# A matmul-bound expert layer on one core: SyncE's transfers are ordered behind the product that precedes them in the source

## The chip, the core and the metric

The kernel runs on one core of one Trainium2 chip. The core has a matmul engine (TensorE, PE in the profile; its weight loads are listed apart as PEld), three engines for elementwise work (VectorE or DVE, ScalarE or ACT, GpSimd or POOL) and SyncE (SP), which here only issues DMA transfers. Each engine takes its instructions in one fixed order. Where an instruction needs another engine's result it waits on a semaphore, and everything behind it on that engine waits too. The metric is the device time of one execution in microseconds (us).

## The reference

The input x has 8 rows of 512 positions with 256 features. There are eight experts and one shared expert, each a gated MLP of width 1024. All in float32, cut to what is computed:

```
for e in 0..7 and the shared one:
    H_e   = silu(x @ Wg[e]) * (x @ Wu[e])        # 8 x 512 x 1024
    out_e = H_e @ Wd[e]                          # 8 x 512 x 256
mixed = sum over e < 8 of gates[b, e] * out_e
out   = x + (1 - s[b]) * mixed + s[b] * out_shared
```

`gates` and `s` hold one number per row b (and expert); they sit in the tile `coef`.

## The kernel before

**Units.** The eight rows are taken in two halves of four (`h`), the nine experts in turn (`e`), and the 1024 hidden features in two halves (`g`). That gives 2 x 9 x 2 = 36 *units*. A unit holds four rows and four blocks of 128 hidden features, so for the gate (m = 0) and the up matrix (m = 1) it has 4 x 4 results of 128 x 512, each over 256 features, two products of depth 128. The kernel spares some of these: for each of the six pairs (i, j) in `PAIRS` it gets the two results (i, j) and (j, i) from three products instead of four. It uses differences and sums of the operands for that. The forms of x (`v`, a difference, and `b`, two sums) come from scratch tensors in DRAM in nearly all units; the forms of the weights (`u`, `wb`, `at`) are made by GpSimd in each unit. The down projection is treated in the same way (`ud`, `wd`, `ad`; `rows` and `cols` are sums of hidden tiles that GpSimd adds up, line 579).

**The order on the matmul engine** is written out by hand as a string for each unit:

```
HUB = "GGD" * 8
BLOCK = "GGDGGDGGD"
ORDER = HUB + BLOCK * 6
```

G is one gate or up product of this unit (`gate_up`, lines 831 to 916), D one down product (`down`, lines 608 to 731). The D's of the *hub* and the first D's after it still belong to the unit before. The hub does the four "diagonal" results (`P_step`, `Q_step`). Block p (p = 0 to 5) then does pair p: for m = 0 and m = 1 it has `R1_step` of pair p + 1 (line 542, uses `v` and `u`) and two `R_step`s of pair p (line 552, use `b` and `wb`). A unit has 26 D's; I number them D1 to D26. D8 ends the hub and D11, D14, D17, D20, D23 and D26 end blocks 0 to 5.

**Where the transfers stand in the source.** All of them after the start are issued on SyncE:

- `x_difference(u, p + 3)`, line 298: `v` of pair p + 3, at the start of block p. Three buffers.
- `x_sums(u, p + 2)`, line 315: `b` of pair p + 2, right after the last `R_step` of block p. Two buffers, so it waits for that product.
- `load_w(nxt, p - 2)`, line 362: for p = 2 to 5, at the start of block p, the next unit's gate and up weights of feature block p - 2, as two transfers (gate first, then up). Five buffers of a tile `w`, four of which a unit holds.
- `make_at(nxt, p - 2)`, lines 369 to 385, directly behind it in the source for p = 3 and 4: GpSimd makes `at` from the weights just asked for.
- `load_d(nxt)`, line 409, at the start of block 5. The first transfers of a unit (`v` of pairs 0 to 2, `b` of pairs 0 and 1) stand at the start of its hub.

**Side jobs.** Two generators run along with the units; each `next` moves one a step. `prepare(1)` (lines 234 to 282) builds the forms of the second half's x in units 2 to 16. A step is taken after D8, D11, D14, D17 and D20 (`AHEAD_AT`); each of the four rows takes six steps (the first issues eight strided loads, line 173) and each of the six pairs eight steps (the first issues two loads of 512 KB, line 265, the eighth three stores of 256 KB, line 280). `close_rows(0)` (lines 754 to 797) finishes the first half's output from unit 20 on, a step after D5, D8, ..., D23 (`CLOSE_AT`): loads of kept sums (lines 762, 769, 771), VectorE operations on them (lines 775 to 792), four strided loads of x (line 738) and four stores (line 796) per row. Both use tiles of a pool of two buffers, `iopool`.

**Who sets the order.** TensorE's and GpSimd's instructions keep the source's order (`HAND`, line 942); ScalarE's do so in unit 0. Everything else is put in order by a planner that plays the program through with its own durations: each time an engine is free in that plan, it takes the first instruction in source order that is ready and whose buffer is free. So a SyncE transfer takes its place in SyncE's queue as soon as the plan has a buffer for it, however far ahead of its place in the source. The order is then fixed, and semaphores are put in where data or buffers need them.

Of the kernel before, what the change touches and what calls it, by code (L numbers as in the profile page):

```python
# [16 lines left out]
def kernel(  # L17
# [37 lines left out]
    nc = tc.nc  # L55
    B, S, D = x.shape
# [4 lines left out]
    NI = 4  # L61
# [35 lines left out]
    gp = nc.gpsimd  # L97
    ve = nc.vector

    def weights(e):  # L100
        return (Wg[e], Wu[e], Wd[e]) if e < E else (Sg, Su, Sd)

# [20 lines left out]
    scratch = {}  # L123
# [23 lines left out]
    def load_rows(pool, tag, b):  # L147
        rows = []
        for c in range(2):
            if pool is not iopool:  # L150
                t = pool.tile([P, 2, D], F32, tag=tag, name=f"xin{b}_{c}")
            elif c == 0:
                both = pool.tile([P, NT, D], F32, tag=tag, name=f"xin{b}")
            if pool is iopool:
                t = both[:, 2 * c : 2 * c + 2]
            nc.sync.dma_start(
                t, x[b].rearrange("(p t) d -> p t d", t=NT)[:, 2 * c : 2 * c + 2, :]
            )
            rows.append(t)
        return rows  # L160
# [6 lines left out]
    def load_turned(to, b):  # L167


        at = x[b].rearrange("(c r t) d -> r t c d", r=32, t=NT)  # L170
        for k in (1, 0):
            for q in range(4):
                nc.sync.dma_start(
                    to[k][ts(q, 32)].rearrange("r (t c d) -> r t c d", t=NT, d=32),
                    at[:, :, :, ts(4 * k + q, 32)],
                )
# [57 lines left out]
    def prepare(h):  # L234

        def tile_of(name):
            return iopool.tile([P, 2, S], F32, tag="io", name=f"{name}{h}")

        for i in range(NI):
            to = xdram[h, i] = dram.tile([P, 2, S], F32, tag=f"xd{h}_{i}", name=f"xd{h}_{i}")  # L240
            rows = [
                zpool.tile([P, S], F32, tag="z", name=f"xin{i}_{k}_{h}") for k in range(2)
            ]
            load_turned(rows, NI * h + i)
            yield
            yield
            both = tile_of(f"xt{i}_")
            for k in (1, 0):
                ve.transpose(both[:, k], rows[k])
                if k == 0 and CI[i] != 0.0:  # L250
                    ve.scalar_tensor_tensor(
                        both[:, 0], both[:, 1], -CI[i], both[:, 0], ALU.mult, ALU.add
                    )
                yield
            yield
            for k in (1, 0):
                nc.sync.dma_start(to[:, k], both[:, k])
            yield
        for p, (i, j) in enumerate(PAIRS):
            d = CI[i] - CI[j]  # L260
            to = dram.tile([P, 3, S], F32, tag=f"xs{h}_{p}", name=f"xs{h}_{p}")
            at = {}
            for n in (i, j):
                at[n] = tile_of(f"f{p}_{n}_")
                nc.sync.dma_start(at[n], xdram[h, n])
            yield
            yield
            v, B_i, B_j = at[i][:, 0], at[i][:, 1], at[j][:, 1]
            gp.tensor_tensor(v, v, at[j][:, 0], ALU.subtract)
            if d != 1.0:  # L270
                gp.tensor_scalar(v, v, 1.0 / d, 0.0, ALU.mult, ALU.add)
            yield
            gp.tensor_tensor(B_j, v, B_j, ALU.add)
            yield
            gp.tensor_tensor(B_i, v, B_i, ALU.add)
            yield
            yield
            yield
            for k, made in enumerate((v, B_j, B_i)):
                nc.sync.dma_start(to[:, k], made)  # L280
            scratch[h, p] = to
            yield

    def load_x(h, i):
        xhub[h, i] = xpool.tile([P, 2, S], F32, tag="x", name=f"x{h}_{i}")
        nc.sync.dma_start(xhub[h, i], xdram[h, i])

    def x_difference(u, p):

        i, j = PAIRS[p]  # L290
        v = vpool.tile([P, S], F32, tag="v", name=f"v{u.name}_{p}")
        if (u.h, p) not in scratch:
            d = CI[i] - CI[j]
            ve.tensor_sub(v, xhub[u.h, i][:, 0], xhub[u.h, j][:, 0])
            if d != 1.0:
                nc.scalar.mul(v, v, 1.0 / d)
        else:
            nc.sync.dma_start(v, scratch[u.h, p][:, 0])
        u.V[p] = v

    def x_sums(u, p):


        i, j = PAIRS[p]
        v = u.V[p]
        b = bpool.tile([P, 2, S], F32, tag="b", name=f"b{u.name}_{p}")
        if (u.h, p) not in scratch:
            ve.tensor_add(b[:, 0], v, xhub[u.h, j][:, 1])
            gp.tensor_tensor(b[:, 1], v, xhub[u.h, i][:, 1], ALU.add)
            scratch[u.h, p] = dram.tile(  # L310
                [P, 3, S], F32, tag=f"xs{u.h}_{p}", name=f"xs{u.h}_{p}"
            )
            u.store.append((scratch[u.h, p], v, b))
        else:
            nc.sync.dma_start(b, scratch[u.h, p][:, 1:3])
        u.VB[p] = b

    def store_forms(u):
        for to, v, b in u.store:
            nc.sync.dma_start(to[:, 0], v)  # L320
            nc.sync.dma_start(to[:, 1:3], b)
        u.store = []

    def touch_banks():
# [29 lines left out]
                u.ad, u.Ud, u.Wd = {}, {}, {}  # L354
                units.append(u)

    def load_w(u, i, queue=nc.sync):
        if i not in u.raw:
            u.raw[i] = wpool.tile([P, 2, 2, P], F32, tag="w", name=f"w{u.name}_{i}")
        t = u.raw[i]  # L360
        for m in range(2):
            queue.dma_start(
                t[:, m],
                weights(u.e)[m][:, ts(NI * u.g + i, P)].rearrange(
                    "(k p) f -> p k f", p=P
                ),
            )
# [38 lines left out]
    def load_d(u):  # L406
        t = dpool.tile([P, NI, D], F32, tag="wd", name=f"wd{u.name}")
        r0 = NI * u.g * P
        nc.sync.dma_start(
            t, weights(u.e)[2][r0 : r0 + NI * P].rearrange("(c p) d -> p c d", p=P)  # L410
        )
        u.raw_d = t
# [186 lines left out]
    def keep(u, acc, *keys):  # L599

        for key in keys:
            if key in acc:
                kept[key] = dram.tile(
                    [P, S], F32, tag=f"kept{key[0]}{key[1]}", name=f"kept{key[0]}{key[1]}"
                )
                nc.sync.dma_start(kept[key], acc[key])

    def down(u, acc):

# [123 lines left out]
    def load_back(h, i):  # L733

        if (h, i) not in back:
            xr = iopool.tile([P, S // 32, 2, 32], F32, tag="io", name=f"xr{h}_{i}")
            for q in range(4):
                nc.sync.dma_start(xr[ts(q, 32)], squares(x, NI * h + i, q))
            back[h, i] = xr
        return back[h, i]  # L740

# [12 lines left out]
    def close_rows(h):  # L754
# [4 lines left out]
        for i in range(NI):  # L759
            y = pair_of(f"y{i}")  # L760
            for r in range(2):
                nc.sync.dma_start(y[:, r], kept["bB"[r], i])
            yield
            for p, (k, j) in enumerate(PAIRS):
                if i not in (k, j):
                    continue
                s = (1.0 if i == k else -1.0) / (CI[k] - CI[j])
                vs = pair_of(f"vs{i}_{p}")
                nc.sync.dma_start(vs[:, 0], kept["V", p])
                if p in OWN:  # L770
                    nc.sync.dma_start(vs[:, 1], kept["S", p])
                yield
                yield
                if p in OWN:
                    ve.tensor_sub(vs[:, 0], vs[:, 0], vs[:, 1])
                    if i == k:
                        ve.tensor_sub(y[:, 1], y[:, 1], vs[:, 1])
                    yield
                ve.scalar_tensor_tensor(y[:, 0], vs[:, 0], s, y[:, 0], ALU.mult, ALU.add)
                yield  # L780
# [12 lines left out]
                )  # L793
                yield
            for q in range(4):
                nc.sync.dma_start(squares(out, NI * h + i, q), xr[ts(q, 32)])
            yield

    last_rows = {}
# [17 lines left out]
    def store_rows(j):  # L817
        b = NI * (NH - 1) + j
        for c, xr in enumerate(last_rows[j]):
            for t in (0, 1) if j == NI - 1 and c == 1 else (slice(0, 2),):  # L820
                if j in tails:
                    ve.tensor_add(xr[:, t], tails[j][c][:, t], xr[:, t])
                at = out[b].rearrange("(p c t) d -> p c t d", c=2, t=2)[:, c]
                nc.sync.dma_start(at[:, t], xr[:, t])

    HUB_STEPS = [
        (what[0], int(what[1]), int(what[2]))
# [116 lines left out]
    by_hand.enter_context(  # L944
        tc.manual_schedule(engines=HAND | {mybir.EngineType.Activation})
    )
    load_w(units[0], 0, nc.scalar)
    load_gates()
    touch_banks()
    loaded = []  # L950
# [13 lines left out]
    for u in units:  # L964
# [52 lines left out]
        if u.n + 2 == len(units):  # L1017
            for _ in closing:
                pass
        if u.n == 0:  # L1020
            by_hand.close()
            by_hand.enter_context(tc.manual_schedule(engines=HAND))
        for _ in turning:
# [38 lines left out]
```

## Time and profile before

| | |
|---|---|
| median of three runs | 2451.72 us (2451.71 to 2453.01) |
| the profiled execution's own time: its span, first to last instruction | 2451.5 us, 22846 instructions |
| PE (matmuls) busy | 2433.5 us, 99% |
| POOL busy | 2115.8 us, 86% |
| DVE busy | 1951.8 us, 80% |
| ACT busy | 1248.6 us, 51% |
| chain that ended last | PE 93%, DVE 3%, POOL 2%, DMA 1%, issue 1% |
| DMA | 267.10 MB, 109 GB/s; SyncE's queue 36.4% of 16 engines' span |
| granted TensorE clock | 1.000 |

Rows of the time line have the start, the duration (both in us), the engine, the source line, the operation with output and input tiles, and in brackets the idle time of that engine just before, with what ended it. SPq is SyncE issuing transfers. Rows of waits have the total, how often, and the longest. Rows of transfers have the count, the size and the median from issue to landing.

### The profile page before, as it was taken

Reading aid. Unit: us, or ns where it says so; the run is one execution under the profiler, and the core shown is the slowest. Engines: PE = TensorE matmul, PEld = TensorE weight load, DVE = VectorE, ACT = ScalarE, POOL = GpSimd, SP = SyncE. Lnnn points to the kernel's source line nnn. Section 1 sums busy time; section 2 is a strip of 40 time slices with the busy share of each in tenths; the row PEclk is TensorE's granted clock in tenths of the full one; section 3 lists DMA queues with packets and bytes.
Section 4 is the critical chain, followed back from the end, with each engine's and each line's share of the span. In section 5 each row is a group of like instructions: output and inputs, shape, how many; then the busy total and the mean of one; then the engine's idle time right before and its main releaser. Section 6 shows DMA issues by size and latency. Waiting matters only on the chain.

```text
span 2451.5 us, 22846 instructions
## 1 busy us (share of the span) xinstructions
PE 2433.5 (99%) x5726; PEld 1078.5 (44%) x5726; DVE 1951.8 (80%) x2881; ACT 1248.6 (51%) x2310; POOL 2115.8 (86%) x2339
## 2 busy tenths in 40 slices
PE   9999999999999999999999999999999999999999
PEld 4444444444444444444444444444444444444444
DVE  6777878777777877787787778888878787777787
ACT  4555555554555555555555555454554555555543
POOL 7988888898888989898888888898888888888885
PEclk9999999999999999999999999999999999999999
DMA  4333343343333333334553323434335343233332
GB/s 145 98 106 112 99 116 112 103 133 104 124 109 97 111 104 99 103 112 125 174 160 96 93 85 104 124 94 125 99 103 146 95 120 91 84 89 97 88 93 86
DMA packets 226129, 267.10 MB, mean 109 GB/s; under 512 B 64336, under 2 KB 156752, under 8 KB 226000
## 3 DMA queue, kind: packets, MB, share of 16 engines
q1 hardware_dynamic: 225168, 265.35, 36.4%
q8 instruction: 48, 0.79, 0.1%
q14 instruction: 81, 0.66, 0.1%
q10 hardware_dynamic: 832, 0.30, 0.0%
HBM read 245.14 MB, written 20.45 MB: 108 GB/s over the span
## 4 chain that ended last, share of the span: by engine, by line
PE 93%; DVE 3%; POOL 2%; DMA 1%; issue 1%; ACT 0%; ACTq 0%; SPq 0%; DVEq 0%; POOLq 0%
PE c L552 29%; PE c L542 15%; PE c L487 9%; PE c L464 9%; PE r L655 7%; PE r L693 7%; PE S L639 5%; PE b L639 5%; PE q L655 5%; PE s L655 2%; POOL cols L579 1%; POOL rows L579 1%; DVE h L455 0%; PE tail L812 0%; DVE P L480 0%
## 5 line engine op out<-in xcount | busy, mean ns | idle before, releaser
L552 PE MATMUL c<-b,wb 128*128 128x512 f32 x1720 | 843.7, 592 | 0.6 <-DMA b<-xs 0.6
L450 ACT ACTIVATE sg<-c 128x512 f32<-128x512 f32 x576 | 343.8, 597 | 585.8 <-DVE c L557 351.8
L455 DVE SCALAR_TENSOR_TENSOR h<-sg,coef,c 128x512 f32<-128x512 f32 x576 | 427.4, 742 | 240.5 <-PE c L552 132.7
L552 PEld LDWEIGHTS c<-b,wb 128*128 128x128 f32 x1720 | 326.4, 190 | 411.1 <-issue 389.1
L542 PE MATMUL c<-v,u 128*128 128x512 f32 x860 | 439.4, 592 | 2.0 <-POOL wb L403 1.5
L579 POOL TENSOR_TENSOR rows<-rows,h 128x512 f32<-128x512 f32 x282 | 372.7, 1322 | 0.0
L579 POOL TENSOR_TENSOR cols<-cols,h 128x512 f32<-128x512 f32 x282 | 363.6, 1289 | 0.0
L547 DVE TENSOR_TENSOR c<-D,c 128x512 f32<-128x512 f32 x430 | 297.5, 692 | 72.6 <-ACT sg L450 51.8
L557 DVE TENSOR_TENSOR c<-c,D 128x512 f32<-128x512 f32 x430 | 296.9, 690 | 17.5 <-PE c L552 17.2
L464 PE MATMUL c<-x,w 128*128 128x512 f32 x572 | 274.5, 592 | 0.0
L402 POOL TENSOR_TENSOR wb<-u,wb 128x256 f32<-128x256 f32 x108 | 79.3, 734 | 220.8 <-ACT wb L400 220.8
L542 PEld LDWEIGHTS c<-v,u 128*128 128x128 f32 x860 | 162.7, 190 | 209.1 <-issue 168.9
L568 DVE TENSOR_TENSOR X<-h,h 128x512 f32<-128x512 f32 x213 | 214.3, 1006 | 6.8
L655 PE MATMUL r<-h,wd 128*128 128x512 f32 x426 | 217.6, 592 | 1.3 <-DVE h L455 1.3
L693 PE MATMUL r<-X,ud 128*128 128x512 f32 x426 | 217.5, 592 | 0.0
L497 ACT COPY D<-c 128x512 f32<-128x512 f32 x284 | 166.0, 584 | 96.2 <-DVE h L455 96.2
L487 PE MATMUL c<-x,at 128*128 128x512 f32 x432 | 210.6, 595 | 3.4 <-DVE P L480 3.0
L579 POOL TENSOR_TENSOR rows<-h,h 128x512 f32<-128x512 f32 x144 | 200.0, 1389 | 0.0
L579 POOL TENSOR_TENSOR cols<-h,h 128x512 f32<-128x512 f32 x144 | 187.7, 1304 | 0.0
L470 ACT COPY P<-c 128x512 f32<-128x512 f32 x216 | 125.9, 587 | 109.2 <-PE c L464 104.9
L464 PEld LDWEIGHTS c<-x,w 128*128 128x128 f32 x572 | 108.4, 190 | 136.0 <-issue 111.9
L638 ACT COPY S<-accS 128x512 f32<-128x512 f32 x135 | 79.6, 590 | 147.9 <-DVE accV L626 146.9
(117 smaller groups left out, 3515.2 us busy)
## 6 DMA issues: line engine op xcount, KB each, us to landing
b<-xs SPq DMA_DIRECT2D x209, 512.0 KB, 3.6
v<-xs SPq DMA_DIRECT2D x209, 256.0 KB, 2.7
wd<-in_L_cond_Wd_dram SPq DMA_DIRECT2D x32, 512.0 KB, 5.0
w<-in_L_cond_Wg_dram SPq DMA_DIRECT2D x127, 128.0 KB, 3.5
w<-in_L_cond_Wu_dram SPq DMA_DIRECT2D x127, 128.0 KB, 3.6
f<-xd SPq DMA_DIRECT2D x12, 512.0 KB, 3.5
xs<-f SPq DMA_DIRECT2D x18, 256.0 KB, 2.9
xin<-in_x_dram SPq DMA_DIRECT2D x16, 256.0 KB, 3.5
```

What stands on the lines that cost most here:

```text
L450: nc.scalar.activation(s, bank, AF.Silu)
L455: ve.scalar_tensor_tensor(t, u.sg[i, j], coef[:, u.e, b : b + 1], bank, ALU.mult, ALU.mult)
L464: nc.tensor.matmul(bank, u.raw[i][:, m, 0], xhub[u.h, i][:, 0], start=True, stop=True)
L487: nc.tensor.matmul(bank, u.at[i][:, m], xhub[u.h, i][:, 1], start=False, stop=True, skip_group_check=True,)
L542: nc.tensor.matmul(bank, u.U[p][:, m], u.V[p], start=False, stop=True, skip_group_check=True)
L547: ve.tensor_sub(other, u.Ds[j, m], bank)
L552: nc.tensor.matmul(bank, u.W[p][:, r, m], u.VB[p][:, r], start=False, stop=True, skip_group_check=True,)
L557: ve.tensor_add(bank, bank, u.Ds[j, m])
L579: gp.tensor_tensor(sums[n], u.h_[n, n] if first else sums[n], u.h_[at], ALU.add)
L639: nc.tensor.matmul(po, w, b, start=not full, stop=True, skip_group_check=full)
L655: nc.tensor.matmul(po, w, b, start=True, stop=True)
L693: nc.tensor.matmul(A, u.Ud[p], u.X[p], start=False, stop=True, skip_group_check=True)
```

## The change

Every `nc.sync.dma_start(to, at)` in the kernel becomes `transfer(to, at)`. From the second unit on, `transfer` adds a dependence of the transfer on the last TensorE product traced before it. The dependence is of a kind that the planner honours (the transfer may not be dispatched in the plan before that product) and that leaves no semaphore in the program.

```diff
+    paced = [False]
+
+    def transfer(to, at):
+        ins = nc.sync.dma_start(to, at)
+        if paced[0]:
+            traced = reversed(nc.cur_bb.bb.instructions)
+            product = next(i for i in traced if i.engine == mybir.EngineType.PE)
+            tc.add_manual_dep(
+                ins.ins, product.name,
+                mybir.DependencyInfo(
+                    mybir.DependencyClass.NoSync, mybir.DependencyReason.DATA
+                ),
+            )
+
...
-            nc.sync.dma_start(v, scratch[u.h, p][:, 0])
+            transfer(v, scratch[u.h, p][:, 0])
...
-            nc.sync.dma_start(b, scratch[u.h, p][:, 1:3])
+            transfer(b, scratch[u.h, p][:, 1:3])
...
-    def load_w(u, i, queue=nc.sync):
+    def load_w(u, i, queue=transfer):
...
-            queue.dma_start(
+            queue(
...
         if u.n == 0:
+            paced[0] = True
             by_hand.close()
```

The other transfers (lines 156, 173, 257, 265, 280, 286, 320, 321, 409, 606, 738, 762, 769, 771, 796 and 824) change in the same way. No transfer is added or removed, no size and no buffer changes, and no other engine's instructions are touched.

More of the change, by code (lines that the diff above doesn't have):

```diff
@@ L155, in load_rows @@
                 t = both[:, 2 * c : 2 * c + 2]
-            nc.sync.dma_start(
+            transfer(
                 t, x[b].rearrange("(p t) d -> p t d", t=NT)[:, 2 * c : 2 * c + 2, :]
@@ L172, in load_turned @@
             for q in range(4):
-                nc.sync.dma_start(
+                transfer(
                     to[k][ts(q, 32)].rearrange("r (t c d) -> r t c d", t=NT, d=32),
@@ L256, in prepare @@
             for k in (1, 0):
-                nc.sync.dma_start(to[:, k], both[:, k])
+                transfer(to[:, k], both[:, k])
             yield
@@ L264, in prepare @@
                 at[n] = tile_of(f"f{p}_{n}_")
-                nc.sync.dma_start(at[n], xdram[h, n])
+                transfer(at[n], xdram[h, n])
             yield
@@ L279, in prepare @@
             for k, made in enumerate((v, B_j, B_i)):
-                nc.sync.dma_start(to[:, k], made)
+                transfer(to[:, k], made)
             scratch[h, p] = to
@@ L285, in load_x @@
         xhub[h, i] = xpool.tile([P, 2, S], F32, tag="x", name=f"x{h}_{i}")
-        nc.sync.dma_start(xhub[h, i], xdram[h, i])
+        transfer(xhub[h, i], xdram[h, i])
     def x_difference(u, p):
@@ L319, in store_forms @@
         for to, v, b in u.store:
-            nc.sync.dma_start(to[:, 0], v)
-            nc.sync.dma_start(to[:, 1:3], b)
+            transfer(to[:, 0], v)
+            transfer(to[:, 1:3], b)
         u.store = []
@@ L408, in load_d @@
         r0 = NI * u.g * P
-        nc.sync.dma_start(
+        transfer(
             t, weights(u.e)[2][r0 : r0 + NI * P].rearrange("(c p) d -> p c d", p=P)
@@ L605, in keep @@
                 )
-                nc.sync.dma_start(kept[key], acc[key])
+                transfer(kept[key], acc[key])
     def down(u, acc):
@@ L737, in load_back @@
             for q in range(4):
-                nc.sync.dma_start(xr[ts(q, 32)], squares(x, NI * h + i, q))
+                transfer(xr[ts(q, 32)], squares(x, NI * h + i, q))
             back[h, i] = xr
@@ L761, in close_rows @@
             for r in range(2):
-                nc.sync.dma_start(y[:, r], kept["bB"[r], i])
+                transfer(y[:, r], kept["bB"[r], i])
             yield
@@ L768, in close_rows @@
                 vs = pair_of(f"vs{i}_{p}")
-                nc.sync.dma_start(vs[:, 0], kept["V", p])
+                transfer(vs[:, 0], kept["V", p])
                 if p in OWN:
-                    nc.sync.dma_start(vs[:, 1], kept["S", p])
+                    transfer(vs[:, 1], kept["S", p])
                 yield
@@ L795, in close_rows @@
             for q in range(4):
-                nc.sync.dma_start(squares(out, NI * h + i, q), xr[ts(q, 32)])
+                transfer(squares(out, NI * h + i, q), xr[ts(q, 32)])
             yield
@@ L823, in store_rows @@
                 at = out[b].rearrange("(p c t) d -> p c t d", c=2, t=2)[:, c]
-                nc.sync.dma_start(at[:, t], xr[:, t])
+                transfer(at[:, t], xr[:, t])
     HUB_STEPS = [
@@ L946 @@
     )
-    load_w(units[0], 0, nc.scalar)
+    load_w(units[0], 0, nc.scalar.dma_start)
     load_gates()
```

## The prediction

> **What bounds the kernel now.** I read the page's first part, then who waited for whom on TensorE (from 68 us on, behind unit 0) and on SyncE, then the time line of one ordinary unit.
>
> ```profile
> span 2451.5 us, 22846 instructions
> PE 2433.5 (99%) x5726; PEld 1078.5 (44%) x5726; DVE 1951.8 (80%) x2881; ACT 1248.6 (51%) x2310; POOL 2115.8 (86%) x2339
> ```
>
> ```profile
> PE c L487 <- DVE P L480: 2.3, 5, 1.2
> PE q L655 <- POOL cols L579: 1.9, 1, 1.9
> PE c L542 <- POOL wb L403: 1.5, 1, 1.5
> PE r L655 <- DVE h L455: 1.3, 1, 1.3
> PE c L552 <- DMA b<-xs: 0.6, 1, 0.6
> PE c L542 <- issue: 0.6, 1, 0.6
> PE b L639 <- ACT b L638: 0.3, 1, 0.3
> PE pto L145 <- DVE accB L630: 0.3, 1, 0.3
> PE tail L812 <- DVE xin L752: 0.2, 1, 0.2
> PE c L487 <- DVE f L482: 0.2, 1, 0.2
> ```
>
> TensorE is the bound. Its idle time from 68 us on is the sum of these ten rows, 9.2 us; no product goes away, so that is all this change can win. DMA ends one of the waits, 0.6 us. SyncE itself mostly stands still, in front of a transfer whose buffer is still being read:
>
> ```profile
> SPq L298 <- PE c L542: 1003.8, 183, 20.9
> SPq L315 <- PE c L552: 587.8, 192, 8.6
> ```
>
> **The change part by part.** It removes and adds no instruction: 0 us of issue. It reorders SyncE's queue, with nothing to hold SyncE back at run time but the semaphores that are there already. So a transfer is moved by what it now queues behind: the last transfer in front of it that really waits. In most places that is a `b`, which waits for its block's last product. Here are two blocks of unit 34 on SyncE:
>
> ```profile
> 2324.35 0.91 SPq L362 DMA_DIRECT2D w<-in_L_cond_Sg_dram  x1
> ...
> 2338.96 0.32 SPq L315 DMA_DIRECT2D b<-xs  x1
> 2340.45 0.38 SPq L362 DMA_DIRECT2D w<-in_L_cond_Sg_dram  x1
> ...
> 2344.11 0.34 SPq L298 DMA_DIRECT2D v<-xs  x1
> 2346.69 0.34 SPq L315 DMA_DIRECT2D b<-xs  x1
> 2347.20 0.38 SPq L362 DMA_DIRECT2D w<-in_L_cond_Sg_dram  x1
> ...
> ```
>
> *`b`* stands right behind the product whose end it waits for (2338.96, 2346.69): it stays, 0 us. *`v`* now goes ahead of `b`, and is only used two blocks on; moved behind, it is 2.6 us later (2344.11 to 2346.69), has over one block of 7.7 us left (2346.69 - 2338.96) and lands in 2.7: 0 us. *`wd`, the first `v`s and `b`s of a unit, the x of the second half*: each has at least the hub or two blocks before its use; 0 us.
>
> *The next unit's weights* are the part with a deadline, because GpSimd's `at` stands directly behind them in GpSimd's own order. The three gate halves above (each up half follows directly) belong to feature blocks 1, 2 and 3. In the source block 1's stands at the start of block 3 of pairs, behind the `b` of 2338.96, and block 2's behind the `b` of 2346.69. In the plan the D product is dispatched shortly before that `b`'s buffer is free, so the gate half should slip in front of `b` and the up half come right behind it. Landings and GpSimd:
>
> ```profile
> b<-xs SPq DMA_DIRECT2D x209, 512.0 KB, 3.6
> v<-xs SPq DMA_DIRECT2D x209, 256.0 KB, 2.7
> w<-in_L_cond_Wu_dram SPq DMA_DIRECT2D x127, 128.0 KB, 3.6
> ```
>
> ```profile
> 2341.62 1.20 POOL L383 TENSOR_TENSOR at<-w 128x256 f32<-128x256 f32 x1
> ...
> 2347.31 0.73 POOL L402 TENSOR_TENSOR wb<-u,wb 128x256 f32<-128x256 f32 x1 [2.04 <-ACT wb L400]
> ...
> 2349.92 1.18 POOL L381 TENSOR_TENSOR at<-w 128x256 f32<-128x256 f32 x1
> ```
>
> ```profile
> 2295.30 0.73 POOL L402 TENSOR_TENSOR wb<-u,w 128x256 f32<-128x256 f32 x1 [0.47 <-PE c L552]
> ...
> 2312.90 1.27 POOL L579 TENSOR_TENSOR cols<-cols,h 128x512 f32<-128x512 f32 x1
> ```
>
> ```profile
> 2315.59 1.02 PE L655 MATMUL q<-cols,ad 128*128 128x512 f32 x2
> ```
>
> Block 1: 2338.96 + 0.32 + 3.6 = 2342.9 against 2341.62, 1.3 us late; the idle 2.04 us ahead of the next `wb` takes that up. Block 2: 2346.69 + 0.34 + 3.6 = 2350.6 against 2349.92, 0.7 us late. From there GpSimd has 0.47 us of idle time (2295.30, the unit before) and then the tightest consumer, the product on `cols`: 2315.59 - (2312.90 + 1.27) = 1.42 us. GpSimd may be late by 0.47 + 1.42 = 1.9 us before TensorE stops. So an ordinary unit costs 0 us, with 1.2 us in hand; should that cover go, each microsecond more costs 33 us over the run.
>
> **The side jobs use that cover up.** They stand after the D that closes a block, so ahead of `load_w` in the source, and now push the weights back. One of their transfers should slip in front of `b`; the rest go behind it. Counting steps, this meets block 2's weights (after D20) in units 6 and 14 (two `f` loads), 9 (three stores), 20, 22 and 25 (two loads of 256 KB) and 26 (four strided loads), and block 1's (after D17) in unit 5 (eight strided loads).
>
> ```profile
> 148.30 5.50 SPq L173 DMA_DIRECT2D xin<-in_x_dram  x8
> ```
>
> ```profile
> 1888.93 1.32 SPq L738 DMA_DIRECT2D xr<-in_x_dram  x2
> ```
>
> - Unit 5: seven at 5.50 / 8 = 0.69 are 4.8 us of issue. The weights land 0.3 + 4.8 + 0.4 + 3.6 = 9.1 us behind `b`, wanted 2.7 behind it (2341.62 - 2338.96): 6.4 late, less 2.04 and 1.9: 2.5 us.
> - Unit 26: three at 0.66, so 0.3 + 2.0 + 0.4 + 3.6 = 6.3 against 3.2 (2349.92 - 2346.69): 3.1 late, less 1.9: 1.2 us.
> - Units 6, 9, 14: 512 KB more in the queue. 256 KB more cost 0.9 us (3.6 - 2.7), so 3.9 + 1.8 + 0.3 of issue = 6.0 against 3.2, less 1.9: 0.9 each, 2.7 us. No row shows this queue; bounds are 0 (a buffer comes free too late and the weights go first) and 1.8 each (both loads behind `b`).
> - Units 20, 22, 25: 3.9 + 0.9 = 4.8 against 3.2, 1.6 late, under 1.9: 0.
> - The 1.9 us wait on `cols` stands in the last unit's hub, where no margin is left, so block 2's 0.7 us goes straight to TensorE: 0.7.
>
> Sum of the losses: 2.5 + 1.2 + 2.7 + 0.7 = 7.1 us, from 0.7 to 12.
>
> **The gains.** The close of the first half runs today in four bursts, as its loads were planned far ahead of their steps. Part of a burst on VectorE; behind it an operation of the same line that stands alone, then TensorE's waits in the first burst's stretch (1225 to 1265 us) and in the last but one's (1840 to 1845):
>
> ```profile
> 1542.89 1.19 DVE L775 TENSOR_TENSOR vs<-vs 128x512 f32<-128x512 f32 x1
> ...
> 1544.00 1.75 DVE L777 TENSOR_TENSOR y<-y,vs 128x512 f32<-128x512 f32 x1
> ...
> 1545.67 1.75 DVE L779 SCALAR_TENSOR_TENSOR y<-vs,y 128x512 f32<-128x512 f32 x1
> ```
>
> ```profile
> 1693.23 0.68 DVE L779 SCALAR_TENSOR_TENSOR y<-vs,y 128x512 f32<-128x512 f32 x1
> ```
>
> ```profile
> PE c L542 <- POOL wb L403: 1.5, 1, 1.5
> PE c L542 <- issue: 0.6, 1, 0.6
> PE c L487 <- DVE P L480: 0.6, 1, 0.6
> ```
>
> ```profile
> PE c L487 <- DVE P L480: 1.2, 1, 1.2
> ```
>
> Three operations take 4.7 us within 4.5, and TensorE then waits 1.3 for `h`. The rows on `P`, `f`, `wb`, `h` and "issue" in the list of ten all lie in or just behind such a burst: 2.3 + 0.2 + 1.5 + 1.3 + 0.6 = 5.9 us. With the loads at their steps, a pair's operations come four steps, 31 us, apart from the next pair's. What stays is bounded by 0 and 5.9; I take 2.5, since a step after D5 lies directly ahead of the six `P` operations of the hub, where the first burst cost 0.6. The gain is 3.4, and 0.6 more for the `b` that waited behind side jobs.
>
> The SBUF page of the Trainium skill ("Who interferes with whom") says that a VectorE operation with two SBUF inputs and a GpSimd operation that reads SBUF block one another fully. The 0.68 and 1.75 us of line 779 agree. By that rule spreading saves no blocked time, the 5.9 us stay, and the sum is worse by 3.4.
>
> Sum: 2451.5 + 7.1 - 3.4 - 0.6 = 2454.6. The page's own time and the median differ by 0.2 us. I forecast **2454.5 us**, no change that the measurement can tell (0.2%, 4.9 us).
>
> **The rivals.** (1) *Pacing wins*: the plan puts both weight halves ahead of `b` or the side jobs find no buffer, the bursts dissolve: 2451.7 - 5.9 - 0.6 = 2445.2. For it: bursts and TensorE's waits coincide. Against: side jobs stand ahead of the weights in the source. (2) *Nothing moves*: without semaphores SyncE runs on to its next real wait, as it does now: 2451.7. Against: the weights of 2324.35 cannot stay ahead of the `b` of 2338.96. (3) *Side jobs cost their upper bound and the bursts' waits stay*: 2451.7 + 12 - 0.6 = 2463. (4) *Late weights in every unit, slower*: GpSimd's `at` waits for the up half; from 1.9 us of lateness on, TensorE waits at `cols`. One more 512 KB ahead of it in each unit makes 0.7 + 1.8 = 2.5, so 0.6 x 33 = 20 us: 2472. For it: GpSimd is 86% busy. Against: nothing that size stands there in an ordinary unit.
>
> The Trainium skill's rule to issue a DMA early and wait late (DMA: Bandwidth & Descriptors, "Rules for kernel authors") speaks for (4). The rows agree that lead shrinks; they leave 1.2 us of cover.
>
> **How the numbers follow.** Forecast 0.36, (1) 0.16, (2) 0.16, (3) 0.20, (4) 0.12. Slower by over 0.2%: 0.20 + 0.12 = 0.32; within: 0.36 + 0.16 = 0.52; faster: 0.16. The forecast's own range is 2450 to 2459. Down to 2446 and up to 2466 about 0.2 stays out, half of (1) and (4).
>
> **What would show it.** On SyncE both halves of a pair of weights around the `b` of their block; GpSimd's `at` of block 2 waiting for DMA for 0.5 to 1 us in each unit; TensorE waiting at a product on `cols` in the hubs behind units 5, 6, 9, 14 and 26, and in no others before the last; VectorE's lines 775 to 779 spread over units 20 to 29. It is wrong if TensorE waits in ordinary units, if VectorE or ScalarE run in another order outside the side jobs, or if the 5.9 us stay whole.

## The result, and the profile after

The changed kernel takes **2466.11 us** (median of four runs, 2460.93 to 2466.41) against 2451.72 us: 14.4 us slower, ratio 1.0052, 95% interval 1.004 to 1.0064. The forecast, 2454.5 us and no change that the measurement can tell, is 11.6 us below it; the measured time lies outside the forecast's own range (2450 to 2459) and just beyond the wider one (2446 to 2466). One of the four runs took 5 us less than the other three, and no trace of it was kept. The profiled execution took 2466.41 us, with a span of 2464.6 us; the traces below are read by spans, and by them the change costs 2464.6 - 2451.5 = 13.1 us.

Lines of the source stand 14 further down, and every paced transfer has line 103 now, that of the helper. First lines of the changed kernel's page:

```profile
span 2464.6 us, 22737 instructions
PE 2436.1 (99%) x5726; PEld 1079.2 (44%) x5726; DVE 1961.2 (80%) x2881; ACT 1247.2 (51%) x2310; POOL 2086.1 (85%) x2339
```

What TensorE waited for from 68 us on (total, times, longest):

```profile
PE q L669 <- POOL cols L593: 17.8, 13, 2.4
PE b L653 <- ACT b L652: 1.4, 2, 1.1
PE c L501 <- DVE P L494: 0.8, 1, 0.8
PE pto L159 <- DVE accB L644: 0.3, 1, 0.3
PE tail L826 <- DVE xin L766: 0.2, 1, 0.2
```

Ten rows have become five. `cols` went from 1.9 to 17.8 us in 13 waits. The others went from 7.3 (9.2 - 1.9) to 2.7 us; of the 5.9 us behind the closing bursts at most 1.9 are left (1.1 on `b` and 0.8 on `P`; the other 0.3 on `b` was there before). The bursts are gone: the twelve operations of line 779, now 793, stood in four stretches of 100 us with three in each (from 1200, 1500, 1600 and 1800 us), and now start from 1385 to 1952 us with some in each of seven such stretches. Behind `cols` stands GpSimd, and in front of GpSimd the weights. What GpSimd waited for; before, the same two rows on `at` had 5.8 us in 2 waits and 0.2 in 1:

```profile
POOL wb L416 <- ACT wb L414: 160.7, 90, 2.9
POOL at L397 <- DMA w<-in_L_cond_Wu_dram: 69.6, 28, 7.7
POOL at L395 <- DMA w<-in_L_cond_Wu_dram: 40.6, 24, 5.2
...
```

By these two rows GpSimd waits 110 us for the up weights (L397 is block 1, L395 block 2), 104 more than before, and the idle time ahead of `wb` (220.8 us before) gave 60 of it back. Only 15.9 us more reach TensorE, because the lateness has to outgrow the cover, and it does so in few places. Unit 34, the one the prediction showed, on SyncE:

```profile
2344.00 0.43 SPq L103 DMA_DIRECT2D w<-in_L_cond_Sg_dram  x1
...
2351.35 0.34 SPq L103 DMA_DIRECT2D b<-xs  x1
2351.74 0.43 SPq L103 DMA_DIRECT2D w<-in_L_cond_Su_dram  x1
2352.84 0.37 SPq L103 DMA_DIRECT2D w<-in_L_cond_Sg_dram  x1
2359.08 0.34 SPq L103 DMA_DIRECT2D b<-xs  x1
2359.47 0.43 SPq L103 DMA_DIRECT2D w<-in_L_cond_Su_dram  x1
...
```

and on GpSimd:

```profile
2355.26 0.72 POOL L397 TENSOR_TENSOR at<-w 128x256 f32<-128x256 f32 x1 [1.21 <-DMA w<-in_L_cond_Su_dram]
...
2363.27 0.72 POOL L395 TENSOR_TENSOR at<-w 128x256 f32<-128x256 f32 x1 [0.92 <-DMA w<-in_L_cond_Su_dram]
```

Each gate half goes ahead of `b`, each up half right behind it. `at` starts 3.9 us behind the `b` of its block for block 1 (2355.26 - 2351.35) and 4.2 for block 2, where 2.7 and 3.2 were the times before. Now unit 20, with one side-job step, on SyncE and then on GpSimd:

```profile
1410.45 0.34 SPq L103 DMA_DIRECT2D b<-xs  x1
1410.83 0.43 SPq L103 DMA_DIRECT2D vs<-keptS  x1
1411.38 0.38 SPq L103 DMA_DIRECT2D w<-in_L_cond_Wg_dram  x1
1411.80 0.47 SPq L103 DMA_DIRECT2D w<-in_L_cond_Wu_dram  x1
```

```profile
1416.85 1.27 POOL L395 TENSOR_TENSOR at<-w 128x256 f32<-128x256 f32 x1 [3.13 <-DMA w<-in_L_cond_Wu_dram]
```

Here both halves are behind `b`, the up half is issued 1.35 us behind it, and `at` starts 5.05 us after that: 6.4 behind `b`, 3.2 later than before.

TensorE's wait in the hub behind each unit (rows on `cols` in a window around that hub), against the prediction's price. The third column is how much later than the 3.2 us of before `at` of block 2 starts behind its `b` (for unit 5 `at` of block 1, against 2.7):

| unit | predicted us | `at` late by us | waited us |
|---|---|---|---|
| 5 | 2.5 | 7.7 | 3.3 |
| 26 | 1.2 | 5.2 | 2.9 |
| 6, 9, 14 | 0.9 each | 3.6, 3.5, 4.4 | 1.1, 0.9, 1.9 |
| 20, 22, 25 | 0 | 3.2, 3.9, 2.0 | 1.7, 1.3, 0.5 |
| 17 | not seen | 3.9 | 1.5 |
| 27 | 0 | 1.5 | 0.2 |
| last hub, beyond 1.9 | 0.7 | 1.0 | 0.5 |
| sum | 7.1 | | 15.8 |

Lateness less wait is the cover that a unit really had: 2.3 to 2.6 us in units 6, 9, 14, 17, 22 and 26, and 1.5 in units 20 and 25. The prediction worked out 1.9. Some 0.5 us of the difference is in `at` itself: it took 1.18 us before (2349.92 in the prediction's rows) and takes 0.72 where it starts late (2363.27 above), but not in unit 20, where it takes 1.27.

Behind unit 5's second wait something else comes. TensorE's time line, and the same stretch by windows (busy us of PE, PEld, DVE, ACT, POOL, then the granted clock) beside one behind an equally long wait:

```profile
426.15 1.12 PE L669 MATMUL q<-cols,ad 128*128 128x512 f32 x2 [1.42 <-POOL cols L593]
...
433.50 1.94 PE L669 MATMUL q<-cols,ad 128*128 128x512 f32 x2 [1.92 <-POOL cols L593]
435.23 1.91 PE L556 MATMUL c<-v,u 128*128 128x512 f32 x2
```

```profile
433.00:437.00 4.00, 3.50 (x5) 1.45 (x6) 0.69 (x1) 0.67 (x2) 3.92 (x5) 0.58 0.00 0
1043.00:1046.00 3.00, 3.00 (x8) 1.33 (x8) 0.69 (x1) 0.37 (x1) 2.92 (x4) 1.00 0.00 0
```

A pair of passes takes 1.9 us where it took 1.0: the granted clock is 0.58 on average over these 4 us, and four passes took 3.44 us (433.50 to 436.94) where four at full clock take 1.72: 1.7 us lost. The balance of spans: +15.9 (`cols`) + 1.7 (clock) - 4.6 (the other waits, 7.3 to 2.7) = +13.0, against 13.1.

### The profile page after: what moved, and what is told of

Read it like the earlier page. It is cut to its first block, busy times and chain, and to the rows that moved or that the text cites. A ratio compares the mean times of both kernels' runs of the same rounds, so it can differ in the third digit from the quotient of the medians.

```text
span 2464.6 us, 22737 instructions
## 1 busy us (share of the span) xinstructions
PE 2436.1 (99%) x5726; PEld 1079.2 (44%) x5726; DVE 1961.2 (80%) x2881; ACT 1247.2 (51%) x2310; POOL 2086.1 (85%) x2339
## 4 chain that ended last, share of the span: by engine, by line
PE 81%; POOL 13%; DVE 2%; DMA 2%; issue 1%; SPq 1%; ACT 0%; POOLq 0%; DVEq 0%
PE c L566 27%; PE c L556 13%; PE c L501 7%; PE c L478 7%; PE r L669 6%; PE r L707 6%; PE S L653 5%; PE q L669 4%; PE b L653 4%; POOL cols L593 4%; POOL rows L593 3%; PE s L669 2%; DMA w<-in_L_cond_Wu_dram 1%; POOL u L404 1%; POOL wd L449 1%
## 5 line engine op out<-in xcount | busy, mean ns | idle before, releaser
L582 DVE TENSOR_TENSOR X<-h,h 128x512 f32<-128x512 f32 x213 | 229.8, 1079 | 6.6
```

Of the source, the lines that this page charges most:

```text
L582: ve.tensor_sub(u.X[p], u.h_[j, i], u.h_[i, j])
```

## The experiments

**Theory after the result:** the loss is the next unit's weights, which stand behind the side jobs' transfers; the gain of the dissolved bursts is real and hidden under it. **Rivals:** the side jobs' own work, done at its steps, makes GpSimd late (A); the `v` and `b` loads that start later do (B). Runs of one group share a chip and 27 runs of the kernel before; its medians there were 2451.32 us (first four runs), 2452.20 (next four) and 2452.29 (last three). The changed kernel was not run again in them, so a difference from its 2466.1 us also carries the 5.5 us by which its own four runs differ.

In four runs the helper paces only some kinds of transfer; the two calls of `load_w` pass "w", the calls in `prepare`, `close_rows` and `load_back` pass "side":

```diff
-    def transfer(to, at):
+    def transfer(to, at, kind="unit"):
         ins = nc.sync.dma_start(to, at)
-        if paced[0]:
+        if paced[0] and kind != "w":
```

**All but the weights paced** (the diff above).

> Every transfer paced as in the changed kernel, but not the loads of the next unit's gate and up weights (`load_w`). Theory (the loss is these weights, pushed behind the transfers of the side jobs, through GpSimd's `at` to the product on `cols`): TensorE's waits on `cols` fall from 17.8 us to under 5 us, the waits behind the closing bursts stay away, 2447.5 us (2445 to 2451). Rival A (the side jobs' own work, done at their steps, makes GpSimd late): the 17.8 us stay, 2463 us or more. Rival B (it is the `v` and `b` loads that now start later): the same, 2460 us or more.

Measured 2447.27 us, ratio to before 0.9983 (0.9974 to 0.9991). TensorE's row on `cols`:

```profile
PE q L671 <- POOL cols L595: 2.8, 2, 1.9
```

Theory holds, A and B fall: side jobs, `v` and `b` are all paced, and 18.8 us go with the weights set free.

**Only the side jobs paced** (`kind == "side"`).

> Only the side jobs' transfers paced (the preparation of the second half's x and the close of the first half's rows). Theory: all of the gain is here (closing work spread out, TensorE's 5.9 us behind the bursts shrink to about 2) and none of the loss, because the weights are free: 2447.5 us (2445 to 2450). Rival A (the side jobs' work at their steps makes GpSimd late): 2460 us or more. Rival C (the gain comes from the other transfers): 2451.7 us.

Measured 2448.11 us, ratio 0.9987 (0.9978 to 0.9997), as expected. Within a microsecond of the run before it, so pacing `v`, `b` and `wd` is worth nothing that can be told.

**Only the weights paced** (`kind == "w"`).

> Only the weight loads paced, all else free as before the change. Theory: their lateness alone (`at` 1.0 to 1.5 us later in an ordinary unit) is covered by GpSimd's idle time and the 1.42 us of margin, the last unit pays 0.5 us, and the bursts' waits come back with 5.9 us: 2452.5 us (2451 to 2456), TensorE waiting at `cols` 5 us or less. Rival (the weights are late in themselves, side jobs or not): `cols` keeps 12 us or more, 2460 us or more.

Measured 2463.76 us, ratio 1.005 (1.0038 to 1.0063): a clear miss of 11 us. The profiled run, 2460.77 us, is the fastest of the five, so 3 us of the miss stand in no trace. In it `cols` has 6.9 us where at most 5 were expected. Its row, and the longest wait of SyncE around the worst place (845 to 870 us):

```profile
PE q L671 <- POOL cols L595: 6.9, 4, 2.5
```

```profile
SPq L103 <- DMA xs<-f: 9.3, 2, 4.8
```

The ordinary units are as the theory has them: behind units 1 to 6 TensorE waits nowhere, as behind 19 to 21. The four waits are behind units 12, 17 and 27, and in the last hub; a stretch of slow clock behind another wait, at 1260 us, costs 1.7 us more. At 856 us the unpaced load of `f` holds SyncE until the stores out of its buffer have landed, and the weights stand behind it, no longer far ahead (GpSimd's `at` then waits 6.1 us for them):

```profile
856.21 0.32 SPq L103 DMA_DIRECT2D f<-xd  x1
856.58 0.42 SPq L103 DMA_DIRECT2D v<-xs  x1
857.10 0.38 SPq L103 DMA_DIRECT2D w<-in_L_cond_Wg_dram  x1
857.57 0.42 SPq L103 DMA_DIRECT2D b<-xs  x1
858.04 0.42 SPq L103 DMA_DIRECT2D w<-in_L_cond_Wu_dram  x1
```

So side jobs push late weights whether they are paced or not. This was formed from the miss, and tested:

**Only the weights paced, written one product earlier.** `load_w` moves from the start of a block to the end of the one before, ahead of its last product, with which a side job's step comes:

```diff
                 if p >= 2:
-                    load_w(nxt, p - 2)
                     if p < 5:
                         make_at(nxt, p - 2)
...
                             sums(p + 2)
+                        if nxt is not None and 1 <= p < 5:
+                            load_w(nxt, p - 1)
                     yield
```

> As the run in which only the weights are paced, which took 2463.8 us where 2452.5 were expected, but with the weights written one product earlier. Theory (there the weights stood behind side jobs' transfers that hold SyncE until a buffer comes free; the lateness of an ordinary unit costs nothing): 2452 us (2450 to 2455), the bursts' waits of before still there. Rival (the dependences of the weights disturb the plan as a whole): 2460 us or more.

Measured 2454.85 us, ratio 1.001 (1.0001 to 1.0019): 9 us of the miss go, as the theory has it, and 2.65 us above before stay. In its profiled run TensorE waits 1.0 us for a `b` and 1.8 us for ScalarE, and a slow stretch follows the wait in the last hub; which of these makes up the 2.65 us is not settled.

**The changed kernel with the weights written one product earlier**, all transfers paced (the same diff).

> The changed kernel, every transfer paced, with the weight loads of the next unit written one product earlier in the source, ahead of the product with which a side job's step comes. Theory: the weights then go right behind or ahead of the `b`, and no side job's transfer is in front of them; `at` waits at most 1.5 us more than before, `cols` 4 us or less: 2448 us (2446 to 2451). Rival A or B (not the weights' place in the queue): 2460 us or more, `cols` still over 12 us.

Measured 2447.43 us, ratio 0.9982 (0.9973 to 0.999): 0.18% faster than before. Unit 20 on SyncE:

```profile
1391.20 0.37 SPq L103 DMA_DIRECT2D w<-in_L_cond_Wg_dram  x1
1391.62 0.46 SPq L103 DMA_DIRECT2D w<-in_L_cond_Wu_dram  x1
1397.43 0.34 SPq L103 DMA_DIRECT2D b<-xs  x1
1397.82 0.42 SPq L103 DMA_DIRECT2D vs<-keptV  x1
1398.29 0.42 SPq L103 DMA_DIRECT2D vs<-keptS  x1
```

What TensorE waited for in it:

```profile
PE q L669 <- POOL cols L593: 1.9, 1, 1.9
PE r L669 <- DVE h L469: 1.3, 1, 1.3
PE c L501 <- DVE P L494: 1.2, 1, 1.2
...
```

Both halves lead `b` by 6.2 and 5.8 us, the side job stands behind, and `cols` is back at its 1.9 us. One product earlier in the source makes a difference of 18.7 us.

**Which block's weights.** The same move for one feature block alone (`p - 1 == 2`, then `p - 1 == 1`).

> The changed kernel with the weights of feature block 2 alone written one product earlier; those of block 1 stay behind the side jobs. By the changed kernel's trace, block 2's `at` behind a side job's transfers sets the stall in units 6, 9, 14, 17, 20, 22, 25 and 26 (13.8 us together), block 1's in unit 5 (3.7 us and a slow stretch behind it). Theory (lateness of block 1 is first taken up by 2 us of idle time ahead of `wb`): those eight stalls go, unit 5's stays: 2452.5 us (2450 to 2455). Rival (block 1's lateness uses the cover up in the units where both come, 6, 14, 17, 22): 6.6 us of it stay, 2459 us.

> The mirror image: the weights of block 1 alone written one product earlier, those of block 2 behind the side jobs. Theory: only unit 5's stall goes, with 0.8 us in units 11, 27 and 29, and perhaps the slow stretch of 1.7 us: 2461 us (2459 to 2463). Rival (block 1's lateness uses the cover up): 6.6 us more goes, 2455 us.

Measured 2452.56 us (1.0003, 0.9994 to 1.0011) and 2458.07 us (1.0028, 1.0019 to 1.0037). Moving block 2's weights wins 13.6 us and lands on the theory's number, in part by luck: by the table the eight waits are 11.8 us, not 13.8, and unit 5's are 3.3. In its trace all eight are gone and unit 5's are 2.6 us, as the theory has it, but 1.9 us came in behind unit 11, and three stretches of slow clock cost 5.1 us; that profiled run took 2456.74 us, 4 more than the median. Moving block 1's wins 8.0, between theory (5) and rival (11): behind units 6, 17 and 22 each of TensorE's waits is 0.6 to 0.8 us shorter and behind unit 26 1.8, so there block 1's lateness was carried into block 2's; of unit 5's waits 0.6 us stay. Together 21.6 us against 18.7 for both; the 2.9 us between them are less than the spread of the changed kernel's own runs, so that they are counted twice is not shown.

**More in front of the weights, in every unit.**

```diff
                 if p >= 2:
+                    if p == 4 and u.n:
+                        for k in range(2):
+                            spare = dram.tile([P, S], F32, tag=f"spare{k}", ...)
+                            transfer(spare, scratch[u.h, k][:, 0])
                     load_w(nxt, p - 2)
```

> The changed kernel with two more copies of 256 KB within device memory in each unit, in the source right ahead of the weights of block 2, so that each ordinary unit looks like unit 20 or 25 (one transfer ahead of the last `b`, one behind it). Theory (cover of 1.9 us, 1.0 us of it used in an ordinary unit): `at` 2 to 3.2 us late, TensorE waits 0.75 to 2.0 us at `cols` in each of 33 units: 2510 us (2485 to 2540). Rival (the stalls come from what the side jobs do on GpSimd and VectorE, not from the place in the queue): within 5 us of the changed kernel, 2461 to 2471 us.

Measured 2494.65 us, ratio 1.0175 (1.0157 to 1.0192): 28.5 us over the changed kernel, 15 below the middle of what was expected. SyncE and GpSimd in unit 2, and TensorE's row:

```profile
193.11 0.34 SPq L103 DMA_DIRECT2D b<-xs  x1
193.49 0.50 SPq L103 DMA_DIRECT2D spare<-xs  x1
194.11 0.53 SPq L103 DMA_DIRECT2D w<-in_L_cond_Wg_dram  x1
194.68 0.47 SPq L103 DMA_DIRECT2D w<-in_L_cond_Wu_dram  x1
```

```profile
198.62 0.72 POOL L395 TENSOR_TENSOR at<-w 128x256 f32<-128x256 f32 x1 [2.24 <-DMA w<-in_L_cond_Wu_dram]
```

```profile
PE q L669 <- POOL cols L593: 30.8, 25, 2.8
```

Here `at` is 5.5 us behind `b` (198.62 - 193.11), 2.3 later than before, and TensorE does not wait behind this unit. It waits behind some units that do no side job, such as unit 33, where `at` is 6.5 us behind the `b` of 2310.59, 3.2 later than before:

```profile
2317.06 0.73 POOL L395 TENSOR_TENSOR at<-w 128x256 f32<-128x256 f32 x1 [3.20 <-DMA w<-in_L_cond_Su_dram]
```

```profile
2347.33 1.12 PE L669 MATMUL q<-cols,ad 128*128 128x512 f32 x2 [0.71 <-POOL cols L593]
```

No engine has more work, so rival A falls here too. The cover is a real edge, but not at 1.9 us. Behind the thirteen units whose `at` is 1.8 to 2.5 us late TensorE does not wait; behind units 32 and 33, 2.8 and 3.2 late, it waits 0.4 and 0.7 us. So the edge lies at about 2.4 us, as in the table above, and the theory's wait in each of 33 units became a wait behind 20 of them, and in the last hub. That is why the time is below the middle of the range. In the profiled run, with 2489.02 us the fastest of the four, TensorE's waits are 14.4 us longer than in the changed kernel and two more stretches of slow clock cost 3.4; where the rest of its 22.6 us of span lies was not found.

**Where the gain comes from.** The side jobs' calls split: `prepare` passes "prepare", `close_rows` and `load_back` pass "close"; one kind is paced.

> Only the transfers of the first half's close (`close_rows`, `load_back`) paced. Theory (the gain is the dissolved closing bursts, 5.9 us of TensorE's waits behind them before, about 2.5 left): all of the gain of the run that paces all side jobs, 2448 us (2446 to 2450). Rival (the gain comes from the preparation's transfers, in front of which a `b` no longer waits): 2451.5 us.

> The counterpart: only the transfers of the second half's preparation (`prepare`) paced. Theory: the bursts stay and TensorE's 5.9 us behind them with them, at most 0.6 us is won: 2451 us (2450 to 2453). Rival: 2448 us.

Measured 2449.35 us (0.9990, 0.9981 to 0.9999) and 2450.43 us (0.9992, 0.9983 to 1.0001). The intervals overlap: by the times, that the gain is the close's alone isn't shown. By the traces, TensorE's 5.9 us behind the bursts (rows on `P`, `f`, `wb`, `h` and "issue") are 2.7 with the close alone paced and 4.9 with the preparation alone. With the close, late weights take part of it back (3.7 us on `cols`, 1.8 of it new).

**A version beyond both.** The weights one product earlier, and the close's steps behind other D's:

```diff
-    CLOSE_AT = (5, 8, 11, 14, 17, 20, 23)
+    CLOSE_AT = (8, 11, 14, 17, 20, 23, 26)
```

> The changed kernel with the weights written one product earlier (2447.4 us), and the close's seven steps of a unit moved behind the 8th, 11th, 14th, 17th, 20th, 23rd and 26th D in place of the 5th to the 23rd. Theory (a step behind the 5th D lies right ahead of the six `P` operations of the hub and costs TensorE 1.2 us at 1835 us, a late load 1.3 us at 1409 us): both go, 2445 us (2443.5 to 2447). Rival (VectorE's extra work is late wherever it stands): 2447.5 us or more.

Measured 2447.52 us, ratio 0.998 (0.9971 to 0.9988): faster than before, no faster than without this move. That is outside the theory's range and the rival's number. The waits of 1.3 and 1.2 us are gone from its trace, as the theory said; three of 0.8 us in sum on `c`, and 0.5 on `P`, came in, and no gain is left that the runs can tell.

## Why the prediction was right or wrong

The forecast was no change that can be told; the kernel is slower by 14.4 us. The mechanism was named (late weights, GpSimd's `at`, the product on `cols`), but the side jobs' term was too small.

- **The bound, and the edits at 0.** Right: the span's 13.1 us are TensorE's waits and a clock, no work. The page counts 109 instructions fewer (22737 after 22846), with the same number of operations on each of the engines.
- **`b`, `v`, `wd` at 0.** Right: `v` takes 3.8 us to land in place of 2.7, and no wait of TensorE ends in a transfer; pacing them or not moved nothing that can be told.
- **Gate half ahead of `b`, up half right behind it, an ordinary unit at 0.** Right in the numbers: `at` was to start 3.9 us behind `b` in both blocks and starts 3.9 and 4.2 behind; there is no wait behind the ordinary units. The cover of 1.9 us was too small a figure (about 2.4 in most units, 1.5 in two), which did no harm here. Rival (4) is out for this kernel; its 20 us for 512 KB more in each unit stand beside 28.5 measured for two copies of 256 KB, and not all units waited.
- **The gains, 3.4 + 0.6 = 4.0 us.** Right: 4.6 by the trace. By the prediction's use of the rule on the SBUF page of the Trainium skill ("Who interferes with whom") the 5.9 us would have stayed. Line 779 (793 now) does take as long one by one as in bursts, 1195 ns on average after 1156. The two lines beside it in a burst became shorter (775: 967 ns after 1182; 777: 949 after 1335), so spreading saved 3 us of the three lines' 28.7 as well. The page does not say that spreading saves nothing; that was my inference, and it failed. That the time still lost falls into VectorE's idle time fits, but no run isolates it.
- **The side jobs, 7.1 us: the step that failed**, by 15.8 - 7.1 = 8.7 us and a slow clock of 1.7. The units of the price list stalled as named (5, 6, 9, 14 and 26); that no others would was wrong (17, 20, 22, 25 and 27). Unit 9's exact 0.9 us is luck: it was 3.5 us late, not 2.8, and had 2.6 of cover, not 1.9. Four terms were too small. First, "one of their transfers should slip in front of `b`" held, but the gate half no longer did: it is issued behind, as unit 20 shows. There the side job's load and the gate half take 1 us of issue ahead of the up half (1410.83 to 1411.80), for which the sum had nothing. Second, a landing was taken as 3.6 us, or 4.5 behind 256 KB; in unit 20 `at` started 5.05 us after the issue. These two turn the 1.6 us of lateness of units 20, 22 and 25, held under the cover, into 2.0 to 3.9. Third, strided loads were priced at 0.69 and 0.66 us of issue, from rows of before, where they were issued at another place; in units 5 and 26 they took 5.88 / 7 = 0.84 and 4.66 / 3 = 1.55 (why so long in unit 26, no run shows):

```profile
386.55 5.88 SPq L103 DMA_DIRECT2D xin<-in_x_dram  x7
...
1819.36 4.66 SPq L103 DMA_DIRECT2D xr<-in_x_dram  x3
```

  Fourth, unit 17 wasn't looked at. It stores the kept sums, and a store also waits, here 1.5 us for VectorE, with the weights behind it:

```profile
1207.85 0.34 SPq L103 DMA_DIRECT2D b<-xs  x1
1209.76 0.32 SPq L103 DMA_DIRECT2D keptV<-accV  x1
1210.17 0.39 SPq L103 DMA_DIRECT2D w<-in_L_cond_Wg_dram  x1
```

- **The rivals.** (3) is nearest in time, 2463, but not in its course: the side jobs went beyond its upper bound of 12 us, and the bursts' waits did not stay. (1), pacing wins, is what the kernel does once the weights are out of the way: 2447 against its 2445.2.

The rule of the Trainium skill that stood behind rival (4), to issue a DMA early and wait for it late (DMA: Bandwidth & Descriptors, "Rules for kernel authors"), agrees with the runs: 18.7 us for one product more of lead. What the lead buys here is the place ahead of the side jobs' transfers.

## What to carry to other kernels

Pacing transfers to the source trades lead for order: it is worth having for work that runs far ahead of its use, and it turns every transfer with a deadline into one that queues behind whatever stands before it in the source. Put the transfers that somebody waits for first in the source, then pace. Price a lateness against the cover of each unit, which differed here between 1.5 and 2.6 us, and take landing and issue times from rows in which the queue is as full as it will be.

## What the hardware showed that was not expected

After a wait of TensorE of no more than 1.9 us the granted clock can fall to half (0.50 over 434 to 436 us in the changed kernel) for some 3.5 us, and 1.7 us are lost beyond the wait. Ten of the thirteen profiled runs have such a stretch, two of them three; the kernel before and the runs with the close alone and the preparation alone have none. So 1.7 us between two profiled runs can be this alone. It came behind unit 5 in the changed kernel (0.58 over 433 to 437 us) and not behind unit 14 (1.00 over 1043 to 1046), both 1.9 us long. The last hub's wait of 1.9 us had it in the run with the weights first and not in the run with the close alone; their windows:

```profile
2378.00:2382.00 4.00, 4.00 (x7) 1.66 (x6) 0.69 (x1) 1.24 (x3) 3.84 (x7) 0.57 0.02 4
```

```profile
2380.00:2384.00 4.00, 4.00 (x10) 1.85 (x11) 1.77 (x3) 2.08 (x4) 3.91 (x5) 1.00 0.38 131
```

So equal waits are followed by the one or the other. The Trainium skill (TensorE: Matmul & The Clock Gate, "Part 1: The HAM clock gate (the "warmup" mystery)") has the clock at half rate after an idle window of about 3.4 us, in windows that run free of the kernel. The half rate and the length agree; the idle time that sets it off is shorter here. That the place of the wait in such a window decides would fit both windows above; no run here shows it.
